# A graph kernel's opening in a new order: loads, a mean on TensorE, and the decoding of the edge list

## Chip, cores and metric

The kernel runs on one core of a Trainium2 chip. The metric is the device time of one launch in microseconds (us). Three runs of the kernel before gave 1735.3, 1740.54 and 1742.44 us; the median is 1740.54.

## What is computed

The reference applies two graph layers to 2,500 nodes of 1,024 features with 80,000 edges sorted by their target node `dst`, everything in float32:

```python
h = relu(layernorm(x))
support = h @ W0                                             # 2500 x 1024
x = x + segment_sum(support[src] * edge_weight[:, None], dst)
h = relu(layernorm(x))
h = h @ W1.T + b1
deg = 1 + (edges that leave a node); norm = deg[row]**-0.5 * deg[col]**-0.5
x = x + segment_sum(norm[:, None] * h[col], row)             # row = src and self, col = dst and self
```

Here `layernorm` has no learned scale. The change touches only the start: the normalisation and product of the first row tiles (`support`) and the decoding of the edge list.

## The kernel before

The nodes are cut into 20 row tiles of 128 (NT = 20), the 1,024 features into 8 chunks of 128 (KC = 8). The edges are cut into 675 blocks of at most 128 edges that all belong to one target tile.

**First product.** The host passes x also transposed. For each row tile the kernel loads its rows `xt` (L152) and its columns `hT` (L161). `moments` (L130 to L136) takes mean and variance from `xt` on VectorE. `transposed_rows` (L164 to L175) builds a diagonal matrix of the means, multiplies it with ones on TensorE (L172) so that each node's mean lies along the columns, subtracts it from `hT` (L173), and applies Relu on ScalarE (L174). The scale 1/std is positive, so it is applied only when the product is read out of PSUM (`products`, L287 to L293). A tile's product (L282) is two column halves of 8 matmuls each, and a matmul of float32 is two records in the profile. The weights `w` come in two halves (L185): the first behind tile 0's loads, the second behind tile 1's.

**Decoding the edge list.** Since `dst` is sorted, the kernel finds where each target tile's edges begin. It loads every block's first `dst` (`heads`, L179), compares them with the tile limits (L205 to L210), adds up over the partitions on TensorE (L212), gathers for each tile the one block in which the tile begins (`there`, L218, an indirect DMA on GpSimd's queue), counts within it (L222 to L225), and spreads the result over the partitions on TensorE (L229). Some small VectorE steps (L231 to L241) turn it into the positions from which six indirect DMAs gather the edges (`got`, L254). These are converted (`got_f`, L311 to L313), transposed on TensorE (L314) and copied out (L316, L319), into target row, source and weight of each edge. Then come about 24 us of VectorE arithmetic (L342 to L402) that make a `key` for each edge.

**Counting and what follows.** With keys and weights the kernel builds one-hot matrices (L446, L448) and counts the edges between each pair of tiles by TensorE (L450). For the four thickest target tiles it also builds weighted matrices, whose factors ScalarE makes (L455). This runs beside the products of tiles 2 to 19. After it, those four tiles are summed by dense products (L632), the others by gathering `support` rows (L592) and multiplying with one-hot matrices (L604). The second layer's product (L577) is mixed in, and the last stage (L794) multiplies by the counts.

**What sets the order.** The author writes instructions in a program order. A scheduler then sorts each engine's queue by priority in that order and by modelled readiness, so a later instruction can be queued ahead of one that isn't ready by its model. An `order_behind(i, other)` adds an edge that only fixes the order. From tile 4 on, counting steps are dealt out between matmuls by a planner in the file (`takes`, L477, and `count`, L513) that adds up estimated costs of TensorE, VectorE and ScalarE. DMAs of SP's queue are issued in the order of that queue. PSUM tiles named `pT` have two buffers, shared by all the small matmuls and transposes of the opening.

GpSimd sets constant tables in the opening: `total` (L245), `second` (L329, L333), `roof` (L336), `wide` (L384) and `iota16` (L405).

Of the kernel before, what the change touches and what calls it, by code (L numbers as in the profile page):

```python
# [9 lines left out]
F32 = mybir.dt.float32  # L10
# [3 lines left out]
I32 = mybir.dt.int32  # L14
U8 = mybir.dt.uint8
AF = mybir.ActivationFunctionType
ALU = mybir.AluOpType
DVE = mybir.EngineType.DVE

P = 128  # L20
# [27 lines left out]
def direct(  # L48
# [26 lines left out]
    nc = tc.nc  # L75
    N, D = x.shape
    E = src.shape[0]
    NT = -(-N // P)
# [69 lines left out]
    def load_rows(t, pool):  # L148
        xt = pool.tile([P, D], F32, name="xt")
        if rows(t) < P:  # L150
            nc.vector.memset(xt, 0.0)
        nc.sync.dma_start(xt[:rows(t), :], x[t * P:t * P + rows(t), :])  # L152
        return xt


    def load_tile(t):
        xt = load_rows(t, sup)
        hT = sup.tile([P, KC, P], F32, name="hT", bufs=AHEAD + 1)
        if rows(t) < P:
            nc.gpsimd.memset(hT, 0.0)  # L160
        nc.sync.dma_start(hT[:, :, :rows(t)], xT[:, t * P:t * P + rows(t)].rearrange("(k p) n -> p k n", p=P))  # L161
        return xt, hT

    def transposed_rows(xt, hT):  # L164
        mv = moments(xt, sup)
        rstd = sup.tile([P, 1], F32, name="rstd")
        nc.scalar.activation(rstd, mv[:, 1:2], AF.Sqrt, bias=eps)
        nc.vector.reciprocal(rstd, rstd)
        diag = sup.tile([P, P], F32, name="diag", bufs=2)
        nc.vector.tensor_scalar(diag, ident, mv[:, 0:1], None, op0=ALU.mult)  # L170
        ps = psum.tile([P, 4, P], F32, name="pT")
        nc.tensor.matmul(ps[:, 0, :], ones, diag, start=True, stop=True)  # L172
        nc.vector.tensor_tensor(hT, hT, ps[:, 0:1, :].to_broadcast([P, KC, P]), op=ALU.subtract)  # L173
        nc.scalar.activation(hT, hT, AF.Relu)  # L174
        return hT, rstd  # L175

    AHEAD = 4
    heads = prep.tile([BP, BC, 1], I32, name="heads")
    nc.sync.dma_start(heads, dst.rearrange("(p c e) -> p c e", p=BP, e=P)[:, :, 0:1])  # L179
    w0_sb = [wpool.tile([P, D], F32, name=f"w{k}") for k in range(KC)]  # L180
    loaded = {}
    for t in range(AHEAD):
        loaded[t] = load_tile(t)
        for k in range(KC) if t < 2 else ():
            nc.sync.dma_start(w0_sb[k][:, t * H:(t + 1) * H], w0[k * P:(k + 1) * P, t * H:(t + 1) * H])  # L185
    ready = {t: transposed_rows(*loaded.pop(t)) for t in range(2)}


# [4 lines left out]
    kio = prep.tile([P, QC], F32, name="kio")  # L193
    nc.gpsimd.iota(kio, pattern=[[P, QC]], base=0, channel_multiplier=1, allow_small_or_imprecise_dtypes=True)
    from_tile = prep.tile([P, QC, NT], F32, name="from_tile")
    last = prep.tile([P, 2, NT], F32, name="last")
    for t in range(NT):
# [5 lines left out]
    nc.vector.tensor_scalar(tile_row, tile_row, -1.0, float(P), op0=ALU.add, op1=ALU.mult)  # L203
    heads_f = prep.tile([BP, BC], F32, name="heads_f")
    nc.vector.tensor_copy(heads_f, heads.rearrange("p c o -> p (c o)"))  # L205
    below = prep.tile([BP, NT, BC], F32, name="below")
    nc.vector.tensor_tensor(below, heads_f[:, None, :].to_broadcast([BP, NT, BC]),
                            tops[:BP, :, None].to_broadcast([BP, NT, BC]), op=ALU.is_lt)
    cnt = prep.tile([BP, NT], F32, name="cnt")
    nc.vector.tensor_reduce(cnt, below, axis=mybir.AxisListType.X, op=ALU.add)  # L210
    ps = psum.tile([P, 4, P], F32, name="pT")
    nc.tensor.matmul(ps[:NT, 0, :2], cnt, ones[:BP, :2], start=True, stop=True)  # L212
    block = prep.tile([NT, 1], F32, name="block")
    nc.vector.tensor_scalar(block, ps[:NT, 0, 0:1], -1.0, 0.0, op0=ALU.add, op1=ALU.max)
    block_i = prep.tile([NT, 1], I32, name="block_i")
    nc.vector.tensor_copy(block_i, block)
    there = prep.tile([NT, P], I32, name="there")
    nc.gpsimd.indirect_dma_start(  # L218
        out=there, out_offset=None, in_=dst.rearrange("(k e) -> k e", e=P),
        in_offset=bass.IndirectOffsetOnAxis(ap=block_i[:, 0:1], axis=0))  # L220
    there_f = prep.tile([NT, P], F32, name="there_f")
    nc.vector.tensor_copy(there_f, there)  # L222
    start = prep.tile([NT, 1], F32, name="start")
# [4 lines left out]
    ps = psum.tile([P, 4, P], F32, name="pT")  # L228
    nc.tensor.matmul(ps[:, 0, :NT], ones[:NT, :], spread, start=True, stop=True)  # L229
    delta = prep.tile([P, NT], F32, name="delta")  # L230
# [13 lines left out]
    total = lay.tile([P, NT, P], F16, name="total")  # L244
    nc.gpsimd.memset(total, 0.0)  # L245
    bias = lay.tile([P, D], F32, name="bias")
# [5 lines left out]
    for c in range(QC):  # L252
        n = min(P, NBP - c * P)
        nc.gpsimd.indirect_dma_start(  # L254
            out=got[:n, c].rearrange("p e q -> p (e q)"), out_offset=None, in_=table,
            in_offset=bass.IndirectOffsetOnAxis(ap=edge_i[:n, c:c + 1], axis=1))
    for t in range(2, AHEAD):
        ready[t] = transposed_rows(*loaded.pop(t))

# [4 lines left out]
    last_count = None  # L264
    fences = []

    def on_pe(i):
# [5 lines left out]

    def order_behind(i, other):
        tc.add_manual_dep(i.ins, other.ins.name,
                          mybir.DependencyInfo(mybir.DependencyClass.NoSync, mybir.DependencyReason.SCHED_ONLY),
                          reason="order of the steps")

    def product(vT, ws, mm):
        for h in range(2):  # L280
            for k in range(KC):
                on_pe(nc.tensor.matmul(mm[:, h, :], vT[:, k, :], ws[k][:, h * H:(h + 1) * H],  # L282
                                       start=(k == 0), stop=(k == KC - 1)))
                if k % 2:
                    yield

    def products(t):  # L287
        hT, rstd = ready.pop(t)
        mm = psum.tile([P, 2, H], F32, name="mm")
        yield from product(hT, w0_sb, mm)  # L290
        row = sup.tile([P, D], F32, name="row", bufs=2)
        nc.scalar.activation(row, mm.rearrange("p h d -> p (h d)"), AF.Copy, scale=rstd)
        nc.sync.dma_start(support[t * P:t * P + rows(t), :], row[:rows(t), :])  # L293

    for t in range(2):
        for _ in products(t):
            pass

    got_f = prep.tile([P, 2, QC, P], F32, name="got_f")
    for i, to in enumerate((row_p, src_p, wgt_p)):  # L300
        for c0 in range(0, QC, 4):
            ps = psum.tile([P, 4, P], F32, name="pT")
            m = min(4, QC - c0)
            for c in range(c0, c0 + m):
                n = min(P, NBP - c * P)
                if i == 2:
                    v = got[:n, c, :, 2].bitcast(F32)
                else:
                    v = got_f[:n, i, c, :]
                    if i == 0:  # L310
                        nc.vector.tensor_scalar(v, got[:n, c, :, i], tile_row[:n, c:c + 1], None, op0=ALU.subtract)  # L311
                    else:
                        nc.vector.tensor_copy(v, got[:n, c, :, i])  # L313
                nc.tensor.transpose(ps[:, c - c0, :n], v, ident[:n, :n])  # L314
            whole = sum(NBP - c * P >= P for c in range(c0, c0 + m))
            nc.vector.tensor_copy(to[:, c0:c0 + whole, :], ps[:, :whole, :])  # L316
            for c in range(c0 + whole, c0 + m):
                n = NBP - c * P
                nc.vector.tensor_copy(to[:, c, :n], ps[:, c - c0, :n])  # L319
# [8 lines left out]
    second = prep.tile([P, NBP - K0[2]], F32, name="second")  # L328
    nc.gpsimd.memset(second, 0.0)  # L329
    for t in range(2, NT):  # L330
        n = TILE_BLOCKS[t] // 2
        v = second[:, K0[t] - K0[2]:K0[t] - K0[2] + 2 * n].rearrange("p (n g) -> p n g", g=2)
        nc.gpsimd.memset(v[:, :, 1], 1.0)  # L333
    roof = prep.tile([P, NBP], F32, name="roof")
    for t in range(NT):
        nc.gpsimd.memset(roof[:, K0[t]:K0[t + 1]], float(P - WINDOWS[t][1]))  # L336
    first_row = prep.tile([P, NBP], F32, name="first_row")
# [45 lines left out]
    for t in range(NT):  # L383
        nc.gpsimd.memset(wide[:, K0[t]:K0[t + 1]], float(WINDOWS[t][1]))  # L384
    off = prep.tile([P, NBP], F32, name="off")
# [13 lines left out]
    for i in range(2):  # L399
# [4 lines left out]
    iota16 = lay.tile([P, 512], F16, name="iota16")  # L404
    nc.gpsimd.iota(iota16, pattern=[[1, 512]], base=0, channel_multiplier=0,  # L405
                   allow_small_or_imprecise_dtypes=True)

# [732 lines left out]
```

## Time and profile before

| what | value |
|---|---|
| profiled execution | 1733.96 us |
| its span | 1732.0 us |
| three timed runs, median | 1740.54 us |
| first product matmul (L282) begins | 13.89 us |
| tile 0's product read out (L292) begins | 37.67 us |
| tile 1's product read out begins | 51.88 us |
| `there` issued, and used | 22.99 us, 28.50 us |
| first edge gather (`got`) issued | 32.44 us |
| last `got` used by VectorE | 45.85 us |
| first one-hot of the counting (L446) | 78.54 us |
| GpSimd's next work after the edge gathers | 389.41 us |

Times inside the execution count from the start of the span. In a row of the timeline the first number is the start, the second how long the row lasted (from the first to the end of the last if it stands for several), then engine, source line, operation, what is written and what is read, and in brackets the idle time before it with what ended it. A row of the table by stretches gives, for each engine, the busy time within that stretch and, in parentheses, its instructions.

### The profile page before, as it was taken

The numbers are of one execution on the slowest core, as the hardware profiler recorded it, in microseconds if no ns is written. First come the engines' busy times: TensorE is split into PE (matmuls) and PEld (weight loads), VectorE is DVE, ScalarE is ACT, GpSimd is POOL, SyncE is SP. The second block draws the span as 40 slices with busy tenths as digits, with TensorE's granted clock in tenths as the row PEclk, the third lists the DMA queues.
The fourth block names the chain that finished last, engine by engine and source line by source line (L and its number), as shares of the span: only waits on it lengthen the run. The fifth ranks groups of instructions, "written<-read, shape, count | busy, mean of one in ns | idle before, by whom it ended". The sixth has DMA issues, their size and how long they took to land. (4 is left out here: it accounts for less than half of the span.)

```text
span 1732.0 us, 21214 instructions
## 1 busy us (share of the span) xinstructions
PE 1654.1 (96%) x6506; PEld 1030.8 (60%) x6506; DVE 1200.3 (69%) x3051; ACT 907.9 (52%) x1476; POOL 525.6 (30%) x501
## 2 busy tenths in 40 slices
PE   6999999999999999999999999998999899999997
PEld 2466555554445555655555555654564678888886
DVE  5788888888889999999999999996772510000000
ACT  3399999982236765665555556664553421111110
POOL 3000000000057776775555556664530000000000
PEclk9999999999999999999999999999999999999999
DMA  7512212123399999998988899898875663433320
GB/s 249 188 62 65 89 53 60 54 68 92 79 364 330 384 317 323 331 362 281 308 286 282 282 322 331 318 333 297 264 265 134 210 164 91 107 79 105 93 65 32
DMA packets 213584, 351.57 MB, mean 203 GB/s; under 512 B 115354, under 2 KB 134820, under 8 KB 213462
## 3 DMA queue, kind: packets, MB, share of 16 engines
q0 software_dynamic: 60592, 219.74, 36.2%
q1 hardware_dynamic: 152870, 130.39, 24.8%
q8 instruction: 54, 0.88, 0.2%
q14 instruction: 68, 0.56, 0.1%
HBM read 282.41 MB, written 54.56 MB: 195 GB/s over the span
## 5 line engine op out<-in xcount | busy, mean ns | idle before, releaser
L598 ACT ACTIVATE hi<-msg,wgt_p 128x1024 fp32r<-128x1024 f32 x378 | 428.6, 1149 | 280.6 <-PE mm L604 180.4
L592 POOL DMA_INDIRECT msg<-support,src_p x378 | 478.0, 1265 | 293.6 <-DVE oh_r L596 90.0
L600 DVE SCALAR_TENSOR_TENSOR lo<-msg,wgt_p,hi 128x1024 fp32r<-128x1024 f32 x378 | 480.1, 1277 | 36.7 <-ACT hi L598 21.1
L604 PE MATMUL mm<-lo,oh_r 128*128 128x512 f32 x756 | 309.8, 491 | 13.2 <-DVE lo L600 13.0
L282 PE MATMUL mm<-w,hT 128*128 128x512 f32 x640 | 318.4, 609 | 2.4 <-ACT hT L174 2.4
L577 PE MATMUL pT<-w,vT 128*128 128x512 f32 x640 | 312.4, 597 | 0.0
L604 PE MATMUL mm<-hi,oh_r 128*128 128x512 f32 x756 | 273.5, 442 | 0.7 <-ACT hi L598 0.7
L455 ACT ACTIVATE wl<-oh_low,wpart 128x128 bf16<-128x128 bf16 x891 | 262.2, 420 | 0.0
L794 PE MATMUL mm<-hi,bT 128*128 128x512 f32 (+1 forms) x800 | 247.6, 392 | 4.6 <-ACT bT L776 2.0
L794 PE MATMUL mm<-lo,bT 128*128 128x512 f32 (+1 forms) x800 | 247.7, 392 | 3.3 <-DVE lo L768 3.3
L782 DVE SCALAR_TENSOR_TENSOR rows<-mm,dis,rows 128x1024 f32<-128x1024 f32 x20 | 25.7, 1283 | 307.9 <-PE mm L794 307.8
L604 PEld LDWEIGHTS mm<-lo,oh_r 128*128 128x128 f32 x756 | 137.9, 189 | 129.3 <-DVE lo L600 51.1
L448 DVE TENSOR_SCALAR oh_key<-iota,key 128x200 bf16<-128x200 f16 (+12 forms) x675 | 194.4, 290 | 5.0 <-PE cb L462 4.9
L776 ACT CAST bT<-cT 128x2560 fp32r<-128x2560 f16 x20 | 46.6, 2335 | 261.0 <-PE mm L794 257.7
L604 PEld LDWEIGHTS mm<-hi,oh_r 128*128 128x128 f32 x756 | 139.3, 189 | 64.2 <-issue 30.2
L794 PEld LDWEIGHTS mm<-hi,bT 128*128 128x128 f32 (+1 forms) x800 | 150.4, 189 | 37.9 <-ACT hi L766 3.1
L794 PEld LDWEIGHTS mm<-lo,bT 128*128 128x128 f32 (+1 forms) x800 | 150.0, 188 | 38.3 <-DVE lo L768 7.0
L458 DVE TENSOR_TENSOR counts<-cb,counts 128x200 f32 (+13 forms) x296 | 138.5, 469 | 48.0 <-PE cb L450 41.2
L446 DVE TENSOR_SCALAR oh_low<-iota,low 128x128 bf16<-128x128 f16 x675 | 167.2, 251 | 1.4 <-ACT wl L455 1.2
L632 PE MATMUL mm<-msg,dense 128*128 128x512 f32 (+1 forms) x320 | 157.1, 601 | 10.2 <-DMA msg<-support 10.2
L577 PEld LDWEIGHTS pT<-w,vT 128*128 128x128 f32 x640 | 120.9, 191 | 72.6 <-issue 55.5
L282 PEld LDWEIGHTS mm<-w,hT 128*128 128x128 f32 x640 | 109.1, 195 | 65.4 <-issue 59.2
(144 smaller groups left out, 1177.5 us busy)
## 6 DMA issues: line engine op xcount, KB each, us to landing
msg<-support POOLq DMA_DIRECT2D x36, 512.0 KB, 6.8
xt<-in_x SPq DMA_DIRECT2D x34, 512.0 KB, 7.3
cnat<-counts SPq DMA_DIRECT2D x20, 640.0 KB, 5.4
hid_d<-hn SPq DMA_DIRECT2D x20, 512.0 KB, 6.5
rows<-hid_d SPq DMA_DIRECT2D x20, 512.0 KB, 4.4
rows<-x_d SPq DMA_DIRECT2D x20, 512.0 KB, 3.8
hT<-in_xT SPq DMA_DIRECT2D x19, 512.0 KB, 3.7
support<-row SPq DMA_DIRECT2D x19, 512.0 KB, 2.9
```

The source lines that it names most:

```text
L282: on_pe(nc.tensor.matmul(mm[:, h, :], vT[:, k, :], ws[k][:, h * H:(h + 1) * H], start=(k == 0), stop=(k == KC - 1)))
L446: nc.vector.tensor_scalar(oh_low, iota16[:, :P], low[:, k:k + 1], None, op0=ALU.is_equal)
L448: nc.vector.tensor_scalar(oh_key[:, :NT * w], iota16[:, :NT * w], key[:, k:k + 1], None, op0=ALU.is_equal)
L455: nc.scalar.activation(wl[:, i, :], oh_low, AF.Copy, scale=wpart[:, i, k:k + 1])
L458: nc.vector.tensor_tensor(to, cb[:, :NT * w].rearrange("p (t w) -> p t w", w=w), to, op=ALU.add)
L577: on_pe(nc.tensor.matmul(mm, vT[:, k, :], w1_sb[k][:, h * H:(h + 1) * H], start=(k == 0), stop=(k == KC - 1)))
L592: nc.gpsimd.indirect_dma_start(out=msg, out_offset=None, in_=support, in_offset=bass.IndirectOffsetOnAxis(ap=src_p[:, k:k + 1], axis=0))
L598: nc.scalar.activation(hi, msg, AF.Copy, scale=wgt_p[:, k:k + 1])
L600: nc.vector.scalar_tensor_tensor(lo, msg, wgt_p[:, k:k + 1], hi.bitcast(F32), op0=ALU.mult, op1=ALU.subtract)
L604: i = nc.tensor.matmul(sums[:, h, :], oh, v[:, h * H:(h + 1) * H], start=(j == 0 and v is hi), stop=(j == n - 1 and v is lo))
L632: m = nc.tensor.matmul(sums[:, i, :], dense[t][:rows(k), k, :], msg[:rows(k), k - k0], start=(k == 0), stop=(k == NT - 1))
L794: nc.tensor.matmul(mm[:, h, :], bT[:rows(k), k, :], v[:rows(k), h * H:(h + 1) * H], start=(k == ORDER[0] and v is his[k]), stop=(k == ORDE ...
```

## The change

All of it lies in the opening of `direct`.

- **Loads.** SP's queue begins with tile 0's columns `hT0`, then `heads`, w half 0, `hT1`, w half 1, and only then the rows of tiles 0 and 1, then tiles 2 and 3.
- **Means.** Tile 0's means are taken from its columns: eight matmuls with a constant matrix of 1/D add up `hT0` over the features, so the sums lie along the columns already. Subtraction and Relu are cut in two halves. Its `moments` are still taken, for 1/std only.
- **Decoding.** The steps from `heads_f` to the gather of `there` stand ahead of the means; the rest of the decoding stands behind the subtraction. The spreading matmul is placed between the fifth matmul of tile 0's product and its second half.
- **Later tiles.** `transposed_rows` of tiles 1 to 3 stands behind tile 0's product; the mean matmul of tiles 2 and 3 is placed behind the fifth matmul of tile 1's product. The conversions `got_f` are placed behind tile 1's subtraction.
- **Tables.** GpSimd's tables are placed behind the edge gathers.

```diff
+    hT0 = load_columns(0)
     heads = prep.tile([BP, BC, 1], I32, name="heads")
     nc.sync.dma_start(heads, dst.rearrange("(p c e) -> p c e", p=BP, e=P)[:, :, 0:1])
...
-    for t in range(AHEAD):
+    load_w0(0)
+    hT1 = load_columns(1)
+    load_w0(1)
+    loaded = {0: (load_rows(0, sup), hT0), 1: (load_rows(1, sup), hT1)}
+    for t in range(2, AHEAD):
         loaded[t] = load_tile(t)
-        for k in range(KC) if t < 2 else ():
-            nc.sync.dma_start(w0_sb[k][:, t * H:(t + 1) * H], w0[k * P:(k + 1) * P, t * H:(t + 1) * H])
-    ready = {t: transposed_rows(*loaded.pop(t)) for t in range(2)}
...
+    counted = nc.tensor.matmul(ps[:NT, 0, :2], cnt, ones[:BP, :2], start=True, stop=True)
...
+    chosen = nc.vector.tensor_copy(block_i, block)
...
+    nc.vector.memset(part_of, 1.0 / D)
+    ps = psum.tile([P, 4, P], F32, name="pT")
+    for k in range(KC):
+        i = nc.tensor.matmul(ps[:, 0, :], part_of, hT0[:, k, :], start=(k == 0), stop=(k == KC - 1))
+        order_behind(i, counted)
+    for k in range(0, KC, 4):
+        centred = nc.vector.tensor_tensor(hT0[:, k:k + 4], hT0[:, k:k + 4],
+                                          ps[:, 0:1, :].to_broadcast([P, 4, P]), op=ALU.subtract)
+        order_behind(centred, chosen)
+        nc.scalar.activation(hT0[:, k:k + 4], hT0[:, k:k + 4], AF.Relu)
+    ready = {0: transposed_rows(*loaded.pop(0), early=True)}
...
-    nc.vector.tensor_copy(there_f, there)
+    order_behind(nc.vector.tensor_copy(there_f, there), centred)
...
+    def set_later(v, value):
+        order_behind(nc.gpsimd.memset(v, value), gathers)
...
+                if first and (h, k) == (0, 4):
+                    order_behind(spreading, i)
+                elif first and h == 1:
+                    order_behind(i, spreading)
...
+    for _ in products(0):
+        pass
+    for t in range(1, AHEAD):
+        ready[t] = transposed_rows(*loaded.pop(t), behind=(made[-12], made[-5] if t == 2 else None) if t > 1 else None)
+        if t == 1:
+            second_centred = centred
+            for _ in products(1):
+                pass
```

## The prediction

> **What bounds the kernel now.** I read the page's head first, then busy time by stretches, then TensorE's own timeline of the opening, then VectorE's and GpSimd's.
>
> The page's head and its busy row, for the whole span:
>
> ```profile
> span 1732.0 us, 21214 instructions
> ...
> PE 1654.1 (96%) x6506; PEld 1030.8 (60%) x6506; DVE 1200.3 (69%) x3051; ACT 907.9 (52%) x1476; POOL 525.6 (30%) x501
> ```
>
> TensorE is busy all but 77.9 us. Busy time by stretches (columns: PE, PEld, DVE, ACT, POOL, granted clock, DMA share, GB/s):
>
> ```profile
> 0.00:14.00 14.00, 0.91 (x3) 0.61 (x3) 10.94 (x80) 10.68 (x7) 7.56 (x71) 1.00 0.78 257
> 14.00:27.00 13.00, 12.66 (x26) 5.34 (x26) 3.62 (x10) 1.35 (x2) 1.05 (x1) 1.00 1.09 358
> 27.00:38.00 11.00, 8.32 (x15) 4.00 (x16) 5.03 (x21) 0.62 (x2) 4.35 (x5) 0.69 0.38 119
> 38.00:60.00 22.00, 20.35 (x56) 9.35 (x55) 16.02 (x44) 4.90 (x7) 1.40 (x2) 0.92 0.93 303
> ...
> 80.00:100.00 20.00, 20.00 (x88) 10.87 (x88) 10.87 (x46) 20.00 (x56) 0.00 (x0) 1.00 0.17 54
> ```
>
> The first 60 us hold 17.8 us of TensorE's idle time (13.1 + 0.3 + 2.7 + 1.7). From 80 to 380 us ScalarE is full (20.00 of 20) and TensorE nearly so; after that TensorE alone. So an earlier start is worth what it moves both at about 80 us. TensorE in the opening:
>
> ```profile
> 10.69 0.80 PE L172 MATMUL pT<-diag,ones 128*128 128x128 f32 x2 [10.69 <-DVE diag L170]
> 13.89 7.07 PE L282 MATMUL mm<-w,hT 128*128 128x512 f32 x10 [2.40 <-ACT hT L174]
> 20.79 0.38 PE L172 MATMUL pT<-diag,ones 128*128 128x128 f32 x2
> 21.11 0.21 PE L212 MATMUL pT<-ones,cnt 125*20 125x2 f32 x2
> 21.24 5.42 PE L282 MATMUL mm<-w,hT 128*128 128x512 f32 x12
> 29.68 0.58 PE L229 MATMUL pT<-spread,ones 20*128 20x20 f32 x2 [3.02 <-DVE spread L227]
> 30.19 7.45 PE L282 MATMUL mm<-w,hT 128*128 128x512 f32 x10
> ```
>
> A matmul of the program is two records. Ten records took 7.07 and 7.45 us where the clock was low; at full clock they are 0.43 apart, 4.3 us. So the opening also loses 2.8 and 3.2 us to the clock, and 2.1 us more after the 1.65 us pause at 53.6 us, where row_p's transposes wait for a bank (four records 3.45 us instead of 1.72, plus 0.4 for slow transposes). Why L229 stands at 29.7 us:
>
> ```profile
> 3.80 4.37 DVE L205 CAST heads_f<-heads 125x5 f32<-125x5 int32 x1 [1.74 <-DMA heads<-in_dst]
> ...
> 28.50 0.22 DVE L222 CAST there_f<-there 20x128 f32<-20x128 int32 x1 [5.83 <-DMA there<-in_dst,block_i]
> ```
>
> A cast of five columns took 4.37 us, until GpSimd's table memsets ended at 8.13 us, where a larger one (there_f) takes 0.22. Then `below` and `cnt` were queued behind tile 0's steps (13.2 to 13.8 us), L212 behind ten matmul records (21.1), and the gather of `there` was issued only at 23.0 us and used at 28.5.
>
> **The change part by part.**
>
> *Loads.* SP's order becomes hT0, heads, w half 0, hT1, w half 1, xt0, xt1. hT0 is issued at 0.74 us; the gathers of `got` land 3.0 us from issue with quiet queues and 0.2 MB, and 0.3 MB more at 351 GB/s is 0.9 us, so hT0 lands near 4.7 us. heads took 3.06 us alone; behind hT0 I take 4.9 (4.2 if nothing holds it, 6.7 with `there`'s loaded 5.5 us). The sixteen w loads keep SP's pace. By the transfer rates of before, moved 1.1 us forward, half 0 is in at 10.5 us, half 1 at 17.6, xt0 at 19.0, xt1 at 20.3.
>
> *Decoding first.* heads_f, below, cnt at 0.2 + 0.26 + 0.25 us, counted from about 5.7 to 6.3, block and block_i 0.28 with hand-overs: GpSimd issues `there` at 7.0 instead of 23.0. With before's 5.5 us it lands at 12.5.
>
> *Means by TensorE.* Eight matmuls of 128 columns, 16 records, all queued behind counted. The nearest rows are L172: 0.38 us a pair at full clock, and slow weight loads of 0.34 each. So 16 x 0.34 = 5.4 us, from 6.3 to 11.7 (3.0 us if fast). Two half subtractions and Relus (halves of 1.22 and 1.06) in a pipeline put the first product matmul at 11.7 + 0.65 + 0.57 + 0.2 = 13.1 us; before 13.89. The gain at the front is only 0.8 us. The removed step is L172 of tile 0; its statistics now only give rstd for the eviction, which is late enough.
>
> *Spreading.* It stands between k=4 of the first half and the second half. Its VectorE chain (0.22+0.33+0.07+0.15+0.22, behind the subtractions) ends at 14.4 us, before TensorE reaches the place. So the 3.0 us wait goes and so does the clock's second fall. Queued behind this wait is the whole second half; if the chain came after 20 us, TensorE would stand there.
>
> *Clock.* In this trace the clock fell at 29.2 and 56.5 us and rose at 36.0 and 59.9; the start's slow stretch ended at 19.0. All lie on one grid of about 3.41 us, and it rose only at the end of a step that was full (29.68 to 32.6 was not enough). The Trainium skill, page "TensorE: Matmul & The Clock Gate", section "What's actually happening", says about 3.4 us of sustained activity suffice; by it the means warm the clock and the product runs at 13.8 us. But the slow means stream 128 columns (0.215 us) per 0.34 us, 63%, and a pause of 1.4 us follows; the 56.5 row shows the clock falling after a step only half full. I take the rows: the product starts slow, for 5.1 us as before, cost 2.55 us. By the rule the sum is 2.5 us better.
>
> *Tile 0's end.* 13.1 + 32 x 0.43 + spreading 0.4 + L172 of tile 1 0.4 + 2.55 = 30.2 us. Before it ended at 37.6. Tile 1: 13.8 + two L172 of 0.4 = 44.8 against 51.8: 7.0 us earlier. Its means need xt1: 20.3 + bn_stats 1.3, aggregate, root and diag 0.8, so 22.5; then subtract 1.22 and Relu 1.06, covered if L172 stands within the product. Where the diff leaves L172 of tile 1 is open: behind the whole product the 2.8 us lie bare.
>
> *Edge gathers.* delta to edge_i is 1.9 us behind spreading, so they are issued near 22 to 29.5 us instead of 32.4 to 39.7, and land by about 36. They are used at about 45, behind second_centred: no wait.
>
> *GpSimd's tables.* 2.22 + 0.48 + 0.21 + 0.85 + 1.13 + 1.29 + 0.56 = 6.7 us, now near 30 to 37 us. They may hold VectorE's casts of got_f as heads_f was held; 12 casts of 0.3 us are due by 45 us, so 4 us of slack hide it. If that cover went, up to 4.4 us. roof and second are used at 63 and 68 us.
>
> *To the counting.* From the first transpose (51.7) to the first oh_low (78.5) before took 26.8 us, mainly VectorE's. Between nothing and 3.75 us of it (the 1.65 us pause and its slow clock) can go, since VectorE has the gathers and statistics behind it; I take 1.5. Sum: 7.0 + 1.5 = 8.5 us earlier, and as ScalarE and then TensorE are full, it reaches the end.
>
> **The sum.** The profiled execution took 1733.96 us, 1.96 outside its span; 8.5 less is 1725.5. It lay below the median of the three runs, 1740.54; from that, 1732.0.
>
> **Rivals.** *All falls well:* the means do warm the clock and the pause at 53.6 goes whole: 8.5 + 2.5 + 2.25 = 13.3 us, 1727.2. For it: the skill's window; against: the half-full row.
>
> *Tile 1 lies bare:* 2.8 us of pause and on average 1.2 us of slow clock: 4.5 us gained, 1736. For it: L172 of tile 1 now stands later in the program than all of product 0. Against: before, TensorE's queue already held other tiles' L172 between product matmuls.
>
> *`there` comes late.* Before, it landed at 28.5 us, just as the load queue ran dry (28.9). If it waits for that, spreading is at 29.5, TensorE stands 6.5 us and then runs slow (3.15): tile 0 ends at 39.6, tile 1 2.4 us later than before, less 1.5: 1741.5. The Trainium skill, page "DMA: Bandwidth & Descriptors", section "Queues, rings and completion order", has a DMA engine take turns between queues packet by packet; by that `there` needs little over the 3.0 us of a quiet gather, and lands at 10 us instead of 12.5. The row says 5.5. Against waiting for the end: SP itself was held up by then, so what was ahead of `there` was already as deep as it gets.
>
> *Slower, through the gather stage.* The engines' queues aren't in program order (base_i's memset runs at 7.8 us), so another opening can re-sort the long stage from 500 us on. Its price: TensorE was idle 9.2 us from 500 to 600 and 1.4 from 700 to 800. Two more stretches like the first cost 2 x 7.8 = 15.6, net +7, and with the pause at tile 1 +11: 1751. It decides from 8.5 us of new idle on. Against: the plan of dense and gathered steps is untouched.
>
> **How the numbers follow.** Likeliest, 0.50, 1732 (own range 1728 to 1735), half of it beyond the 0.5% (8.7 us) that a measurement of this kernel can tell from none; all well 0.17; tile 1 bare 0.15; late `there` 0.06; gather stage worse 0.12. Faster 0.25 + 0.17 = 0.42, same 0.25 + 0.15 + 0.06 = 0.46, slower 0.12. The range from 1724 to 1745 holds all but the gather case and the edge of the good one.
>
> **What would show it.** Right: heads_f about 0.2 us long, `there` issued near 7, first product matmul near 13, no pause before the second half, tile 0 over at 28 to 31, first oh_low near 70, TensorE's idle time elsewhere unchanged. Wrong: a pause before tile 1's product, or idle time after 400 us that differs by more than 4 us.

## The result, and the profile after

The changed kernel took 1730.96 us (median of 11 runs, 1727.42 to 1736.04), the kernel before 1739.27 us beside it (11 runs, 1732.95 to 1742.89). The ratio is 0.9962, with a 95% interval of 0.9947 to 0.9977: 4.0 to 9.2 us faster. The forecast was 1732.0 us. The profiled executions don't show this by themselves: 1734.97 us after, 1733.96 before. So the two traces are compared by when each stage begins, and the end by the timed runs. Two slow runs, one of the kernel before (1890.08 us) and one of mean1_by_pe (5563.14 us), are left out of the comparisons.

The page's head and its busy row after. TensorE's idle time is unchanged, 77.6 us (1732.7 less 1655.1) against 77.9:

```profile
span 1732.7 us, 21263 instructions
...
PE 1655.1 (96%) x6520; PEld 1034.3 (60%) x6520; DVE 1200.5 (69%) x3052; ACT 908.3 (52%) x1477; POOL 524.1 (30%) x501
```

Busy time by stretches after, the columns as before (the granted clock is the third number from the end):

```profile
0.00:14.00 14.00, 6.68 (x22) 4.82 (x23) 6.32 (x80) 10.60 (x7) 2.24 (x11) 1.00 0.80 240
14.00:27.00 13.00, 13.00 (x32) 5.85 (x31) 6.91 (x24) 0.59 (x2) 5.68 (x6) 1.00 1.07 385
27.00:38.00 11.00, 4.30 (x8) 1.94 (x7) 10.13 (x27) 2.94 (x5) 6.49 (x62) 0.70 1.09 354
38.00:60.00 22.00, 22.00 (x68) 10.91 (x68) 17.06 (x40) 3.52 (x4) 0.00 (x0) 1.00 0.82 282
```

Of the first 60 us TensorE is idle 14.0 now (7.3 + 0 + 6.7 + 0), against 17.8. Apart from the start, what is left of it stands in one piece, at 27 to 38 us. TensorE's timeline shows which:

```profile
6.04 3.79 PE L236 MATMUL pT<-hT,part_of 128*128 128x128 f32 x16
11.27 6.03 PE L310 MATMUL mm<-w,hT 128*128 128x512 f32 x10 [1.44 <-ACT hT L242]
17.23 0.39 PE L261 MATMUL pT<-spread,ones 20*128 20x20 f32 x2
17.55 9.71 PE L310 MATMUL mm<-w,hT 128*128 128x512 f32 x22
27.09 0.38 PE L181 MATMUL pT<-diag,ones 128*128 128x128 f32 x2
```

Tile 0's product runs through, with the spreading (L261) in its middle and no pause; it is read out at 27.56 us instead of 37.67. Then L181, the mean of tile 1, stands behind all of it, and the product of tile 1 begins only at 34.18 us, after a pause of 6.70. VectorE says why so long (L254 is `there_f`):

```profile
4.97 0.17 DVE L216 CAST heads_f<-heads 125x5 f32<-125x5 int32 x1 [2.25 <-DMA heads<-in_dst]
...
14.32 0.21 DVE L254 CAST there_f<-there 20x128 f32<-20x128 int32 x1 [3.17 <-DMA there<-in_dst,block_i]
...
27.36 3.49 DVE L179 TENSOR_SCALAR diag<-ident,mv 128x128 f32<-128x128 f32 x1
...
30.42 1.29 DVE L133 BATCH_NORM_STATS2 stats<-xt 128x6 f32<-128x512 f32 x2
...
31.86 1.18 DVE L187 TENSOR_TENSOR hT<-hT,pT 128x1024 f32<-128x1024 f32 x1
```

`heads_f` isn't held any more: 0.17 us instead of 4.37. But GpSimd's tables run from 27.03 to 33.49 us now, and VectorE's diagonal for tile 2 (L179, 0.29 us when alone) lasts 3.49 us, until the short memsets end at 30.89. Behind it stand tile 3's statistics (L133), and only then tile 1's subtraction (L187) and its Relu. L181 itself was done at 27.47.

So the lead shrinks on the way: 10.1 us at tile 0's read-out, 1.5 at tile 1's (50.40 against 51.88), 3.4 at the first one-hot of the counting (75.16 against 78.54), 4.6 at the last read-out of the first product (467.45 against 472.09). The forecast had 8.5 at the counting and at the end. The timed medians differ by 8.3, so by them about 3.7 us came from behind the first product; their interval, 4.0 to 9.2, doesn't exclude the 4.6 alone. A place for it is in TensorE's groups of 470 to 600 us, before,

```profile
L632 PE MATMUL mm<-msg,dense 128*128 128x512 f32 (+1 forms) x94 | 47.6, 616 | 3.0 <-DMA msg<-support 3.0
L604 PE MATMUL mm<-lo,oh_r 128*128 128x512 f32 x113 | 47.2, 498 | 5.5 <-DVE lo L600 5.4
...
L450 PE MATMUL cb<-oh_key,oh_low 128*128 128x360 bf16 (+1 forms) x48 | 12.2, 336 | 3.7 <-DVE oh_key L448 3.6
```

and after:

```profile
L644 PE MATMUL mm<-lo,oh_r 128*128 128x512 f32 x119 | 50.2, 501 | 7.6 <-DVE lo L640 7.4
L672 PE MATMUL mm<-msg,dense 128*128 128x512 f32 (+1 forms) x96 | 49.2, 619 | 0.6 <-DMA msg<-support 0.4
...
L490 PE MATMUL cb<-oh_key,oh_low 128*128 128x360 bf16 (+1 forms) x39 | 10.1, 326 | 1.5 <-DVE oh_key L488 1.2 <-DVE counts L498 0.2
```

The number behind the second bar is TensorE's idle time ahead of the group. The dense products and the rest of the counting wait 6.7 us before, 2.1 after; the gathered products wait 2.1 us more for `lo`. TensorE's whole idle time in this stretch is 12.9 us before and 11.5 after, and its mean granted clock 0.96 and 0.97. No line of this stage was edited. But the edges of the opening sort TensorE's queue anew, and VectorE's and ScalarE's with it: TensorE's instruction lists in the built programs differ down to entry 3,705 of some 12,050, where the gathered tiles are being summed, and are alike from there on.

### The profile page after: what moved, and what is told of

Read it like the earlier page. It is cut to its first block, busy times and chain, and to the rows that moved or that the text cites. A ratio compares the mean times of both kernels' runs of the same rounds, so it can differ in the third digit from the quotient of the medians.

```text
span 1732.7 us, 21263 instructions
## 1 busy us (share of the span) xinstructions
PE 1655.1 (96%) x6520; PEld 1034.3 (60%) x6520; DVE 1200.5 (69%) x3052; ACT 908.3 (52%) x1477; POOL 524.1 (30%) x501
## 5 line engine op out<-in xcount | busy, mean ns | idle before, releaser
L310 PE MATMUL mm<-w,hT 128*128 128x512 f32 x640 | 313.8, 603 | 8.1 <-ACT hT L188 6.7
```

Of the source, the lines that this page charges most:

```text
L310: i = on_pe(nc.tensor.matmul(mm[:, h, :], vT[:, k, :], ws[k][:, h * H:(h + 1) * H], start=(k == 0), stop=(k == KC - 1)))
```

## Experiments

**Theory.** The opening gives 4 to 5 us; the pause at tile 1 took the rest, because L181 stands behind product 0, the tables hold VectorE, and tile 3's statistics are queued ahead. The other part of the gain is a queue that happened to be sorted better in the gather stage. **Rivals:** the tables alone make the pause, or the place of L181 alone; the whole gain is the opening's.

All times in us. "Remainder" is the timed median less the last read-out of the profile. "Waits" is TensorE's idle time ahead of the dense products and the counting from 470 to 600 us; "idle, clock" is all its idle time in that stretch, with its mean granted clock. "Order" names which kernels share TensorE's queue.

| kernel | tile 1 read out | first one-hot | last read-out | waits | idle, clock | median (runs) | remainder | ratio to before [95%] | order |
|---|---|---|---|---|---|---|---|---|---|
| before | 51.88 | 78.5 | 472.09 | 6.7 | 12.9, 0.96 | 1739.27 (11) | 1267.2 | 1 | A |
| before_tables_late | 53.06 | 76.2 | 469.73 | 6.9 | 13.2, 0.95 | 1738.09 (11) | 1268.4 | 0.9992 [0.9975, 1.0009] | A |
| changed | 50.40 | 75.2 | 467.45 | 2.1 | 11.5, 0.97 | 1730.96 (11) | 1263.5 | 0.9962 [0.9947, 0.9977] | B |
| changed_again | 50.55 | 75.3 | 467.58 | 1.8 | 10.9, 0.99 | 1730.90 (12) | 1263.3 | 0.9956 [0.9938, 0.9974] | B |
| tables_wait | 49.22 | 74.0 | 466.27 | 1.6 | 10.4, 0.97 | 1730.80 (7) | 1264.5 | 0.9952 [0.9935, 0.9969] | B |
| tables_hold | 49.63 | 75.8 | 467.84 | 2.2 | 11.4, 0.97 | 1730.79 (5) | 1263.0 | 0.9958 [0.9942, 0.9974] | B |
| tables_first | 48.15 | 72.9 | 465.20 | 2.2 | 11.4, 1.00 | 1725.49 (6) | 1260.3 | 0.9933 [0.9912, 0.9953] | B |
| sub_first | 47.05 | 71.8 | 464.13 | 0.9 | 8.9, 0.98 | 1728.37 (5) | 1264.2 | 0.9944 [0.9930, 0.9958] | B |
| sub_first_wait | 45.42 | 71.7 | 463.98 | 0.9 | 10.6, 0.98 | 1727.98 (5) | 1264.0 | 0.9938 [0.9924, 0.9951] | B |
| tables_spread | 46.16 | 71.8 | 464.10 | 0.5 | 10.3, 0.99 | 1727.47 (7) | 1263.4 | 0.9937 [0.9914, 0.9960] | B |
| mean_inside | 49.68 | 74.7 | 468.39 | 7.2 | 13.7, 0.96 | 1736.33 (12) | 1267.9 | 0.9982 [0.9967, 0.9997] | C |
| tables_wait_mean_inside | 48.77 | 73.8 | 467.50 | 6.8 | 12.9, 0.97 | 1736.97 (22) | 1269.5 | 0.9990 [0.9982, 0.9998] | C |
| mean1_by_pe | 45.57 | 73.9 | 467.49 | 8.0 | 15.2, 0.95 | 1741.16 (17) | 1273.7 | 1.0015 [1.0002, 1.0028] | D |
| stats_later | 46.23 | 71.6 | 468.41 | 8.9 | 15.4, 0.93 | 1740.88 (12) | 1272.5 | 1.0026 [1.0012, 1.0039] | E |

The kernels ran in groups on several chips, each beside the kernel before (median 1737.1 to 1739.4). Line numbers differ a little between them: the subtraction of L187 is L189 in sub_first, the diagonal of L179 is L181.

### The same kernel once more

changed_again has no edit.

> The changed kernel itself, on the chip and beside the runs of before that the next two kernels have. Expected: the ratio of the first measurement, 0.996, to within 0.002, product 1 near 34 us, the last product's read-out near 467.

It gave 1730.90 us and 0.9956, as the first time. Its profile has a span of 1725.1 us, the first had 1732.7. The openings agree (last read-out 467.58 and 467.45); the last stage begins at 1339.7 and at 1345.9. So a single profile's end scatters by some 7 us, all of it from the gather stage on, while the first product's end repeats within 0.2.

The pause at tile 1 was 5.75 us here, 6.70 there, and VectorE wasn't held for it: GpSimd began its tables at 27.52 us, too late to hold tile 2's diagonal.

```profile
27.35 0.30 DVE L179 TENSOR_SCALAR diag<-ident,mv 128x128 f32<-128x128 f32 x1
...
29.97 1.29 DVE L133 BATCH_NORM_STATS2 stats<-xt 128x6 f32<-128x512 f32 x2 [2.12 <-DMA xt<-in_x]
```

In this execution tile 3's rows alone made the pause, through their statistics ahead of tile 1's subtraction.

### When GpSimd sets the tables

tables_wait makes the tables that `set_later` sets, and iota16, wait for tile 1's subtraction:

```diff
+        i = nc.gpsimd.memset(v, value)
+        order_behind(i, gathers)
+        wait_for(i, second_centred)
```

> The changed kernel, with GpSimd's tables waiting for tile 1's subtraction. Theory (VectorE is held by GpSimd's tables while tile 1 waits for it): tile 2's diagonal, 3.49 us in the changed kernel, takes 0.3; the subtraction of tile 1 begins near 29.4 us instead of 31.9 and its product near 31.8 instead of 34.2; the kernel is 2.4 us faster than the changed one, ratio to before near 0.9948. Rival one (VectorE stood for another reason, a load or the clock): the diagonal stays at 3.5 us and the product begins at 34. Rival two (what the opening gains is eaten in the gather stage): the product begins earlier, but the ratio stays at 0.996.

VectorE in tables_wait:

```profile
26.51 0.29 DVE L179 TENSOR_SCALAR diag<-ident,mv 128x128 f32<-128x128 f32 x1
26.84 0.16 DVE L175 RECIPROCAL rstd<-rstd 128x1 f32<-128x1 f32 x1
29.56 1.29 DVE L133 BATCH_NORM_STATS2 stats<-xt 128x6 f32<-128x512 f32 x2 [2.56 <-DMA xt<-in_x]
...
31.00 1.17 DVE L187 TENSOR_TENSOR hT<-hT,pT 128x1024 f32<-128x1024 f32 x1
```

The diagonal is back at 0.29 us, so the tables did hold it. Yet the pause didn't shrink: 7.49 us, product 1 at 33.32. (Product 0 ended 1.7 us earlier than in the changed kernel, as its first ten records took 4.56 us.) I had expected 4.3 us and 31.8. What failed is that I took the hold for the only cause: with it gone, VectorE stands 2.56 us before tile 3's rows, whose statistics are queued ahead of tile 1's subtraction. Two covers lay over each other. The ratio, 0.9952, can't be told from the changed kernel's.

tables_hold has the same wait on a later step, the first copy of `row_p`:

```diff
+        wait_for(i, copied)
```

> The changed kernel with GpSimd's tables waiting still longer, for the first copy of row_p, so that they fall into VectorE's arithmetic ahead of the counting; all other queues keep their order, so this is a delay by itself. Theory (GpSimd's memsets hold VectorE's casts and one-input arithmetic, and what the opening loses reaches the end whole): the tables run from about 51 to 58 us, the step inside, at 55 in the changed kernel, waits until about 58, the first oh_low comes 3 to 4 us later than with the tables waiting for tile 1's subtraction (74.0), and the time is 3 to 4 us longer than that kernel's, ratio near 0.997. Rival (no hold): oh_low at 74, ratio 0.995. Rival (the later stages absorb it): oh_low at 78, ratio still 0.995.

Tile 1's pause, again without the hold, was 4.88 us: tile 3's rows were there at 28.74 us. The first one-hot came 1.8 us later than in tables_wait (75.8 against 74.0), about half of the 3 to 4 us I had expected. The short memsets let VectorE's casts and copies through; what held the cast `hi_t`, of 0.50 us elsewhere, was the one long memset of `total`:

```profile
56.71 2.22 POOL L290 MEMSET total<- 128x2560 f16 x1
...
57.22 2.08 DVE L426 CAST hi_t<-part 128x675 f32<-128x675 int32 x1
```

The end can't be told apart (0.9958 against 0.9952).

tables_first gives the tables back to GpSimd without any edge, and keeps the rest of the change:

```diff
+    nc.gpsimd.memset(total, 0.0)
-        order_behind(nc.gpsimd.memset(v, value), gathers)
+        nc.gpsimd.memset(v, value)
```

> The changed kernel with GpSimd's tables back at the start, that part alone undone. Theory: heads_f is held again until about 8.1 us, the means begin near 9 instead of 6, tile 0's product near 14.4 instead of 11.3 and ends near 30.3; tile 2's diagonal takes 0.3 us and the pause before product 1 is 2.7 us instead of 6.7, so product 1 begins near 33.0 instead of 34.2: moving the tables bought nothing, this kernel is 0 to 2 us faster than the changed one, ratio 0.995 to 0.9965. Rival one: the pause stays at 6.7 us, product 1 begins near 37, 3 us slower than the changed kernel, ratio 0.998. Rival two: 0.996 whatever the opening.

My expectation of `heads_f` failed: it lasted 0.17 us. Only `total` was set first (1.70 to 3.92 us); the short memsets were queued behind the gather of `there` and ran from 8.16 to 11.92. There they held other VectorE work, and tile 0's subtraction behind it:

```profile
8.37 3.63 DVE L470 CAST counts<-ident 128x128 f16<-128x128 f32 x1
...
11.99 1.27 DVE L239 TENSOR_TENSOR hT<-hT,pT 128x512 f32<-128x512 f32 x2
```

Product 0 began at 13.38 us, 2.1 later than in the changed kernel, and tile 0 was read out at 29.5. But the pause at tile 1 was 2.51 us, and the counting began 2.3 us earlier. A hold isn't removed by moving it. But tile 1 had to wait for tile 3's rows in any case: their statistics began at 28.43 us and product 1 at 32.20, 3.77 behind. In the changed kernel, changed_again, tables_wait and tables_hold it is 3.76 or 3.77 as well. So in all five these statistics set where product 1 begins, and a later product 0 only shortens the pause. This has the lowest median of all, 1725.49, but its interval (0.9912 to 0.9953) overlaps with the changed kernel's.

before_tables_late is the kernel before with this one part of the change, the tables behind the edge gathers:

```diff
+    def set_later(v, value):
+        order_behind(nc.gpsimd.memset(v, value), gathers)
```

> The kernel before with the tables alone moved behind the edge gathers; the queues of TensorE and VectorE keep their order. Theory: heads_f takes 0.2 us instead of 4.4, tile 0's statistics start when its rows land, by 7 us instead of 8.3, and its product about 1.3 us earlier; the wait for there and its clock are unchanged, and the tables now hold got_f's casts from about 40 us, with 5 us of slack: 0 to 2 us gained, ratio 0.999. Rival (the tables' move carried the change's gain): ratio 0.996. Rival (the hold at 40 us is bare): 2 us or more slower, ratio over 1.001.

`heads_f` took 0.17 us at 3.83, and product 0 began at 11.95 us, 1.9 earlier. Then the same hold came up later, at the conversions (L313, 3.23 us at 38.33), with a pause of TensorE that before didn't have:

```profile
42.23 0.49 PE L177 MATMUL pT<-diag,ones 128*128 128x128 f32 x2 [2.84 <-DVE diag L175]
```

Tile 1 was read out 1.2 us later than before, the first product ended 2.4 us earlier. Timed, 0.9992 (0.9975 to 1.0009): nothing that can be measured. This part alone doesn't make the gain.

### What stands ahead of tile 1's subtraction

sub_first places tile 3's statistics behind tile 1's subtraction and leaves the tables as the change has them:

```diff
-            nc.vector.bn_stats(stats[:, h, :], xt[:, h * H:(h + 1) * H])
+            i = nc.vector.bn_stats(stats[:, h, :], xt[:, h * H:(h + 1) * H])
+            if after is not None:
+                order_behind(i, after)
...
+                                   after=second_centred if t == 3 else None)
```

> The changed kernel, with tile 3's statistics queued behind tile 1's subtraction on VectorE instead of ahead of it; the queues of TensorE, SP and GpSimd keep their order. Theory (two covers lie over each other: GpSimd's tables hold VectorE to 30.9 us, and tile 3's rows land near 29.6 to 30.4): with the tables still in the way the subtraction only moves from 31.9 to about 31.0 us, product 1 from 34.2 to 33.3, and the kernel gains at most 1 us on the changed one, ratio to before 0.995 to 0.996. Rival (the load of tile 3 alone is what it waits for): the subtraction begins near 28, product 1 near 30, ratio 0.993.

The pause fell to 4.56 us. Product 1 began at 31.10, between the 33.3 I had expected and the rival's 30. Beside the subtraction and its Relu, what is left is the hold:

```profile
26.15 3.76 DVE L181 TENSOR_SCALAR diag<-ident,mv 128x128 f32<-128x128 f32 x1
...
26.58 3.33 DVE L189 TENSOR_TENSOR hT<-hT,pT 128x1024 f32<-128x1024 f32 x1
```

The subtraction, queued next, ends with the hold, at 29.91.

sub_first_wait joins this edit and that of tables_wait; its diff is the two above.

> Both covers taken away: tile 3's statistics behind tile 1's subtraction, and GpSimd's tables waiting for it; TensorE's order is still that of the changed kernel. Theory: the subtraction begins as soon as TensorE has spread tile 1's means, near 27.2 us at the latest, product 1 near 29.6, and the pause is 2.5 to 2.8 us instead of 6.7; 4.5 us faster than the changed kernel, ratio near 0.993. Rival (each alone suffices): no earlier than with tile 3's statistics moved alone. Rival (the gather stage takes it back): product 1 near 29.6, ratio 0.996.

The pause fell to 2.40 us, product 1 at 30.20. The four kernels make a square: pause 6.70 with both causes, 7.49 without the hold (4.88 in tables_hold, 5.75 in changed_again), 4.56 without the statistics ahead, 2.40 without either. Of the 4.3 us above 2.40 the statistics alone keep 2.5 or more, the hold alone 2.2. By product 1's beginning it is 34.18, 33.32 (32.51 and 33.73), 31.10 and 30.20 us: the statistics are the larger cause. The last 2.4 us are subtraction and Relu themselves behind L181, as the rival "tile 1 lies bare" had priced them, at 2.8.

tables_spread has sub_first's edit, sets `total` and the ground of `second` early, and lets the other tables wait for tile 0's second subtraction:

```diff
+    nc.gpsimd.memset(total, 0.0)
...
+        wait_for(nc.gpsimd.memset(v, value), first_centred)
```

> Tile 3's statistics behind tile 1's subtraction, the table total at the start of GpSimd's queue, second behind the gather of there, and the other tables waiting for tile 0's subtraction: they run near 11 to 15 us, where VectorE waits for there. TensorE's, VectorE's, ScalarE's and SP's queues are those of the kernel with tile 3's statistics moved alone. Theory (tables hold VectorE wherever they meet its casts): product 1 begins near 29.5 us with a pause of 2.5, got_f is not held, the first oh_low comes at 70 to 71 us (71.8 there), and the time is 1 us less than that kernel's, ratio 0.993 to 0.994. Rival (the tables now hold there_f and the spreading matmul): TensorE stands before the second half of product 0, oh_low at 73 or later, ratio 0.995.

The pause was 4.02 us (product 1 at 30.36), and the counting began at 71.8, as in the other two. I had expected 2.5, 29.5 and 70 to 71: `got_f` wasn't held any more (0.29 us), but tile 2's statistics still stood ahead of the subtraction, which began at 28.00. Against the changed kernel the three start the counting 3.4 us earlier and end the first product 3.3 to 3.5 us earlier; their medians are 2.6 to 3.5 us lower. Their intervals overlap with the changed kernel's, so the timed runs allow this gain but don't prove it for each alone.

### The mean of tile 1 elsewhere

mean_inside places L181 of tile 1 between the last matmuls of product 0:

```diff
-... if t > 1 else None)
+... if t > 1 else (made[-3], made[-1]))
```

> The changed kernel with one order edge: tile 1's mean matmul ahead of the last matmul of tile 0's product instead of behind it. By this edge the scheduler sorts the queues of TensorE, VectorE and ScalarE otherwise down to the middle of the gather stage (TensorE's are those of the kernel with waiting tables and the mean inside, entry for entry). Theory (a new sort of the long stages is worth as much as the opening): the opening ends no later than in the changed kernel (product 1 within 1 us of 34, last product read out near 467 to 468), yet the time is 5 to 7 us longer, ratio near 0.999 to 1.000. Rival (only the opening counts): ratio 0.995 to 0.996 as the changed kernel beside it.

Product 1 began at 33.12 us, only 0.6 earlier than in changed_again. VectorE's diagonal was held (2.37 us at 27.28), but what came last was tile 3's rows again: half of their statistics still stood ahead of tile 1's subtraction and began at 30.17, after 0.51 us of waiting for them. The first product's end stood 0.8 us later than there. But the kernel ended 5.4 us later (1736.33 against 1730.90, beside each other on one chip), 0.9982 (0.9967 to 0.9997).

tables_wait_mean_inside joins it with tables_wait; its diff is those two.

> As the kernel with the waiting tables, and tile 1's mean matmul placed between the 13th and the last matmul of tile 0's product; by this order the subtraction of tile 1 also stands ahead of half of tile 3's statistics. Theory: the subtraction begins near 28.4 us, product 1 near 30.8, a pause of 3.7 us instead of 6.7; 3.4 us faster than the changed kernel plus up to 1 us of clock, ratio near 0.994. Rival one: no earlier than 34. Rival two: earlier, ratio 0.996.

Its counting began 0.2 us earlier than in tables_wait, its first product ended 1.2 us later, and it took 1736.97 us against 1730.80: 6.2 us more. I had expected a ratio near 0.994; it was 0.9990.

mean1_by_pe takes the mean of tile 1 as the change takes that of tile 0, by eight matmuls within product 0, and has no L181 for it:

```diff
+    for k in range(KC):
+        i = nc.tensor.matmul(ps[:, 0, :], part_of, hT1[:, k, :], start=(k == 0), stop=(k == KC - 1))
+        order_behind(i, made[9])
+    order_behind(made[10], i)
```

> The changed kernel, with tile 1's means also taken by eight matmuls from its columns, inside tile 0's product (ahead of its 11th matmul), so that its product no longer depends on its rows. Theory: TensorE works 16 records x 0.19 = 3.0 us more, but the pause of 6.7 us goes: product 1 begins near 30.2 and at full clock, and ends near 44.7 instead of 50.3; 5.6 us faster than the changed kernel, ratio near 0.993. Rival one (VectorE is held by something other than the tables): the subtraction lies ahead of the tables, so this doesn't tell. Rival two: product 1 ends near 45, ratio 0.996.

TensorE in mean1_by_pe:

```profile
20.15 1.95 PE L332 MATMUL pT<-hT,part_of 128*128 128x128 f32 x16
...
27.75 6.71 PE L310 MATMUL mm<-w,hT 128*128 128x512 f32 x15 [0.49 <-ACT hT L338]
```

The pause is gone (0.49 us), tile 1 was read out at 45.57 us, nearly the 44.8 that I had forecast for the change, and the first product ended as in the changed kernel (467.49). And this kernel, for which I had expected 0.993, is slower than before: 1.0015 (1.0002 to 1.0028). What it lost, it lost after 467 us.

### A new sort alone

stats_later is tables_spread with one edge more: the statistics of tiles 4 to 6 behind tile 2's subtraction.

```diff
-            ready[t + 2] = transposed_rows(*load_tile(t + 2))
+            ready[t + 2] = transposed_rows(*load_tile(t + 2), after=third_centred if t < 5 else None)
```

> This is tables_spread with one more edge: the row statistics of tiles 4 to 6 are queued behind tile 2's subtraction, where tables_spread has them ahead of it (there VectorE waited 1.52 and 1.50 us for their rows). Theory (each cover taken off shows the next; VectorE's waits for the row loads now set the start of the counting): tile 1's product is read out near 46 us as in tables_spread, and the first one-hot starts about 2 us earlier, near 70 (tables_spread 71.8). Rival (VectorE's arithmetic on the edges alone sets it): 71.8 again. For the end there are two expectations. The edge also sorts TensorE's queue anew between the opening and the gather stage. If only the opening counts, the end follows the start of the counting: about 1726. If a new sort weighs as much, the time from the last read-out of the first product to the end differs from the 1260 to 1264 us of the kernels with the changed kernel's order by more than 4 us in either direction, as in mean_inside (1268) and mean1_by_pe (1274).

The first expectation failed: tile 2's subtraction came 1.4 us earlier (41.93 against 43.28), but the first one-hot at 71.6, not 70. The lead was gone at 55.3 us, where the arithmetic (`first_row`) waited 0.50 us for TensorE's small matmuls and began when tables_spread's did. The second came true. The opening is tables_spread's within 0.2 us, and the end is 13.4 us later, 1740.88 against 1727.47; the intervals, 1.0012 to 1.0039 and 0.9914 to 0.9960, are far apart. The first product ends 4.3 us later, the remainder is 9.1 us longer. TensorE's groups of 470 to 600 us in stats_later:

```profile
L684 PE MATMUL mm<-msg,dense 128*128 128x512 f32 (+1 forms) x91 | 47.7, 629 | 5.2 <-DMA msg<-support 5.2
...
L502 PE MATMUL cb<-oh_key,oh_low 128*128 128x360 bf16 (+1 forms) x43 | 11.3, 328 | 3.7 <-DVE oh_key L500 3.4
```

The same two waits, 8.9 us, that before has with 6.7 and tables_spread with 0.5. At the seam itself, stats_later runs thirteen counting matmuls between the last product and the first dense one, at the pace of VectorE's one-hots, tables_spread eight: 7.1 us from the last read-out to the first dense matmul against 4.8.

Two pairs show that an order edge alone does this: stats_later against tables_spread, and mean_inside against changed_again (5.4 us). The edges sort TensorE's, VectorE's and ScalarE's queues at once, so the runs don't tell which of them it is.

For the changed kernel itself the case is weaker. Across the fourteen profiles the waits are 0.5 to 2.2 us in order B and 6.7 to 8.9 in A, C, D and E, and the remainder is 1260.3 to 1264.5 and 1267.2 to 1273.7. All idle time of 470 to 600 us, plus 130 us times what the granted clock lacks to 1, is 18.1 and 19.7 in A, 11.4 to 15.4 in B, 16.8 to 24.5 in the others. But over the whole gather stage, from the last read-out to the first matmul of the last stage, only C, D and E stand out, with 40.4 to 44.0 us of TensorE idle: B has 33.9 to 37.2 and A 35.6 and 36.1. By the timed runs B gains more on before, beside it, than its lead at the last read-out in all eight kernels, by 1.8 to 6.8 us; but before_tables_late, with the order of before, gains 2.4 less. So B is the better order between 470 and 600 us, and that it is worth 3.7 us at the end isn't shown. No run has the change's opening with the order of before.

## Why the prediction was right, and where it wasn't

**The number** was right (1732.0 against 1730.96), and in part by luck, for **the sum** wasn't: 8.5 us at the counting were really 3.4, then 4.6 at the first product's end, and the 3.7 that the timed runs have beyond that came from where the forecast had none. Of the prediction's own signs, the first one-hot near 70 didn't come, and the pause before tile 1's product, a sign of being wrong, did; idle time after 400 us differs by 1.5 (51.9 and 53.4).

- *Loads, decoding.* Right. `heads_f` at 4.97 us for 0.17 (forecast 4.9 and 0.2), `there` issued at 6.82 (7.0). It was used at 14.32 instead of 12.5: 7.5 us from its issue, where before had 5.5. The turn-taking of queues that the Trainium skill describes ("DMA: Bandwidth & Descriptors", section "Queues, rings and completion order") would have made it about 3; with the load queue full, the row was nearer, and still too low. Nothing waited behind it, as spreading had its cover.
- *Means.* Mis-sized. Sixteen records took 3.79 us, not 5.4, so product 0 began at 11.27 instead of 13.1. Inside product 0 they take 1.95 (mean1_by_pe), so the two records I took for near rows, with their slow weight loads, were no measure.
- *Clock.* I chose the row over the skill's rule ("TensorE: Matmul & The Clock Gate", section "What's actually happening"). In the changed kernel's profile the product's first ten records took 6.03 us, between the two; in tables_spread they took 4.56, at the full pace at once. Of the twelve kernels with the new means seven took 4.56 and five 6.02 to 6.29. So the means can warm the clock, as the rule has it; whether they do differs from run to run. This is read from the records' pace: the granted clock stands at 1.00 from 11.3 to 17.2 us in the changed kernel.
- *Tile 0's end* came at 27.56 instead of 30.2, by these two terms.
- *Tile 1.* Here the sum failed: 7.0 us earlier was 1.5. The step that failed is "covered if L172 stands within the product". It stands behind it (L181 after), the alternative that I had left open and priced at 2.8 us. On top came 3.9 us, for which the sum had nothing: I had asked whether the tables hold the conversions `got_f`, and given them 4 us of slack, but not what else VectorE has to do at 27 us. Tile 3's statistics stand ahead of the subtraction in one queue, and their rows come at 28.4 to 30.5 us; the held diagonal lies over the same wait. And the clock fell in the pause: it was granted at 0.50 from 34.2 to 38.0 us, and tile 1's 22 records took 11.66 us instead of the 9.71 of tile 0's last 22. (After 2.40 us of pause, in sub_first_wait, they took 9.71; after 2.51, in tables_first, 11.41.)
- *To the counting.* From 51.7 to 78.5 before, 50.4 to 75.2 after: 2.1 us shorter, 1.5 forecast.
- *Rivals.* The opening went as "tile 1 lies bare" said, in size too (4.5 us against 4.6 at the first product's end), but that size is luck: the pause was 6.70 us instead of 2.8, and tile 0 was over 2.6 us sooner than forecast. "Gather stage" had the right mechanism: the opening's edges do sort the queue anew down to there. For this change it didn't fall to the bad side; mean1_by_pe and stats_later show that one. Its price for the stage, 15.6 us, was about twice too high: beside before, D and E lose 6.6 and 7.5 us behind the first product.

**Open:** how much of the timed 3.7 us is order B's, and what makes an order good. It comes out of the scheduler's model at build time, and no run here takes it apart.

## What to carry to other kernels

When an edit in the opening changes edges that a scheduler sorts by, compare the queues' orders down to the end before putting the difference down to the edit: here a new sort of the queues was worth 13 us between two kernels with one opening, and the change's opening 4.6. Before costing a step at nothing, list everything in its engine's queue between it and the next thing that others wait for; two covers over each other are seen only by lifting each and both. Don't name a cause from one execution: the same kernel, run again, had the pause without the hold. And measure the last stage that is unaffected by chance: the first product's end repeated within 0.2 us, the whole span didn't within 7.

Four versions have clearly lower medians than the changed kernel, tables_first (0.9933), tables_spread (0.9937), sub_first_wait (0.9938) and sub_first (0.9944); each is faster than before by its whole interval, none is shown to beat the changed kernel by itself.

## What the runs showed of the hardware

- A run of short GpSimd memsets can hold one VectorE operation for the whole run and not for one memset: with 59 of them from 27.03 to 30.89 us, a diagonal that takes 0.29 us lasted 3.49 us, to 30.85. In sub_first and tables_first it was the same (3.76 and 3.63 us). It isn't always so: in sub_first_wait a held conversion was let go at 31.86 us, 1.2 us ahead of the run's end, and in tables_hold casts and copies of VectorE ran between the memsets at 0.18 to 0.69 us each, while GpSimd's last twenty took 1.98 us instead of 1.29. In the kernel before, `heads_f` ended at 8.17 us with iota16 (8.13); the short memsets were over at 7.61.
- One long memset holds as well: in tables_hold a cast of 0.50 us lasted 2.08 us, to 59.30, beside `total` (to 58.93); in sub_first a conversion lasted 2.57 us, to 32.64, beside `total` (to 32.56).
- No run shows statistics (L133) or subtractions that read PSUM held by themselves; they were late because they stood behind a held operation, or ended with it.
- Sixteen records of 128 columns took 1.95 us inside product 0 (mean1_by_pe) and 3.40 to 3.79 at the start of the kernel. The granted clock is 1.00 in both stretches of mean1_by_pe, so this slow start has to be read from the records.
